# Fewer, fuller tiles of distance bounds, and the first inverse roots ahead of a branch, in a four-layer network on one Trainium2 core

## The chip, the core and the metric

The kernel runs on one core of one Trainium2 chip. Its time is the device time of one execution in microseconds. The time before is 2672.19 us, the median of 3 runs (2671.6 to 2673.48). The engines are called by the names that the profile uses: PE (matmuls), PEld (weight loads), DVE (the vector engine), ACT (the scalar engine), POOL, and SP, which issues the DMAs.

## What is computed

The input is a batch of B = 4 images of 56 x 56 tokens of C = 128 channels. Four layers follow each other: a neighbourhood attention with an MLP, a gated linear recurrence, a softmax attention over the 3136 tokens of an image followed by a mixture of 8 experts, and last an attention by distances followed by an expert choice of 64 experts. The change concerns the distance attention most. The reference computes it in this way:

```python
Q, K, V = (projections of the normalised tokens)
q2 = jnp.sum(Q * Q, axis=-1)
k2 = jnp.sum(K * K, axis=-1)
qk = jnp.einsum('bqd,bkd->bqk', Q, K)
dist2 = q2[:, :, None] + k2[:, None, :] - 2.0 * qk
scores = jnp.exp(-GAMMA * dist2)
attn = jax.nn.softmax(scores, axis=-1)
return jnp.einsum('bqk,bkd->bqd', attn, V)
```

Where all distances are large, every score is the exponential of a very negative number, so all weights of the softmax are equal and the layer adds the mean of V to each token. The kernel takes this short way and proves on the chip that it may: for every pair of a query and a key it bounds the distance from below, by 30 of the 128 channels. If one bound is not large enough, a general version of all layers runs after a second branch. With these inputs it doesn't run.

## The kernel before

**Set-up and branch.** `folded_weights` (L2617 to L2711) loads the weights of the first layers, folds the norm's scale and shift into the projections, centres three 128 x 128 weights (`centred`, L2084), multiplies two of them (`product`, L2094), and bounds the scores of the neighbourhood attention and of the softmax attention. The result is one integer, `safe` (L2709). Every engine reads it and branches (L2710, L2895). The loads are all issued by SP, in program order; the seven groups of image 0, `x[0]`, are the last ones in front of the branch (`fetch`, L148 to L153).

**First layer.** `neighbourhood_of_safe_scores` (L471) works on 28 stripes (4 images, 7 groups of 4 tiles of 112 tokens). The order of PE, DVE and ACT in it is written out by hand. It starts with `ahead(0)` and `ahead(1)`: each takes four pairs of statistics on DVE (L551, L552) and then a chain of 13 small DVE instructions, the inverse roots (`inverse_root`, L875, with `roots`, L541). `first_norm` then normalises the group's four tiles on ACT (L583). `tokens` transposes them (L202) and copies them out (L599), `constants` computes exponentials of small tables on ACT (L784, L789) and `pad_v` on DVE (L785), and `keys` and `queries` make the projections. After that come `ahead(2)`, and the loop over stripes with `ahead(3)` to `ahead(5)` in its first round. DMAs of the constants (`band` to `w_fc2`) are issued behind the branch.

**Softmax attention with pieces beside it.** `Attention.run` (L2002) goes through the images. Per image PE does some 175 products of keys and queries (`s_ps`, L1969), ACT their exponentials (L1976), and PE as many products with the values (`o_ps`, L2052), all on 448 columns in fp32. Between these steps it starts pieces of other layers, by a list of pieces with costs that `Paced` (L1566) spreads over the image; a piece that is marked `apart` is the only one of its list in a step. `background` (L2742) says which pieces stand beside which image: the recurrence beside images 0 and 1; the mixture of experts and the distance layer of images 0 and 1 and the bounds of image 0 beside image 2; the bounds of images 1 and 2, and other pieces, beside image 3. Outside the first layer a scheduler orders the instructions of each engine when the program is built, so that the order on an engine is fixed at run time.

**Bounds.** In `FarAttention.image` (L1711) `products(g)` makes, for group g of 448 tokens, the queries `q_near` (30 channels, repeated in the four quarters of the partitions) and the keys `k_near`: the four tiles of 112 keys of group h lie in the four quarters of 32 partitions, side by side in `k_near[:, h, :]`. `with_norms` (L1757) adds the norms to them. `bounds(g, h)` (L1766) then makes four matmuls (L1772), one from each quarter: 32 rows of 112 keys against 448 queries, in bf16, into four PSUM tiles `d_ps` of 112 x 448. Each is reduced to one column: quarters 0 and 2 by a maximum on DVE (L1777), quarters 1 and 3 on ACT (L1783), by a relu with a sum; with `scalar=True` all are on ACT. An image has 7 x 7 calls, so 196 matmuls and 196 reductions; four images have 784. The PSUM tiles come from a pool of four, which the other pieces share.

**End.** `layers_of_safe_scores` (L2718) splits the bounds of image 3 into halves of two matmuls, in an order in which groups become ready (L2807). Some 21 halves stand beside the last pieces of the mixture and the distance layer, on ACT alone. The rest is handed to `ExpertChoice.experts` (L2296), which spreads them over the 16 lots of experts; per lot PE makes `h_ps` (L2318), ACT copies it (L2325), PE transposes it (L2331), DVE adds a bias (L2334), ACT takes the gelu (L2341), and PE makes the output (L2347). The weights of the lots come by DMA, 1 MB at a time. `decide` (L1830) takes the maximum over everything found. `scatter` adds the results to the tokens and writes the output.

Of the kernel before, what the change touches and what calls it, by code (L numbers as in the profile page):

```python
# [9 lines left out]
F32 = mybir.dt.float32  # L10
# [11 lines left out]
GT = 4  # L22
# [99 lines left out]
NR = 4  # L122
KB, QC = 112, 14
# [3 lines left out]
class Env:  # L127
# [20 lines left out]
    def fetch(self, b, parts=1):  # L148

        n = NT // parts  # L150
        src = self.ins["x"][b].rearrange("(t r) w c -> (r w) t c", r=2)
        for t in range(0, NT, n):
            self.nc.sync.dma_start(self.x[b][:, t : t + n, :], src[:, t : t + n, :])  # L153
# [317 lines left out]
def neighbourhood_of_safe_scores(env: Env, f, work):  # L471
# [17 lines left out]
    with ExitStack() as ctx:  # L489
# [64 lines left out]
        def ahead(i):  # L554

            (b, s), (x, tiles) = stripes[i], tiles_of(i)
            all_of = statistics[b]
            if s == 0:
                all_of["mv"] = sp.tile([P, NT, 2], F32, tag="mv_all", name="mv_all", bufs=2)
            for t in range(tiles.start, tiles.stop):  # L560
                statistic(x, t, all_of["mv"][:, t, :])
            if b == 0:
                held[i]["norm"] = roots(all_of["mv"][:, tiles, :], GT)
            elif s == NG - 1:
                rs, off = roots(all_of["mv"], NT)
                for s2 in range(NG):
                    of = slice(s2 * GT, (s2 + 1) * GT)
                    held[b * NG + s2]["norm"] = rs[:, of], off[:, of]
# [248 lines left out]

        plan = work(ps1, NG + 1)
# [8 lines left out]
        with tc.manual_schedule(  # L827
            engines={mybir.EngineType.PE, mybir.EngineType.DVE, mybir.EngineType.Activation}
        ):
            for i in range(2):  # L830
                ahead(i)
                first_norm(i)
# [787 lines left out]
class FarAttention:  # L1620
# [14 lines left out]

    def __init__(self, env, ctx, flow, work):
# [23 lines left out]
        self.far = cp.tile([P, 1], F32, tag="far", name="far")  # L1660
        self.half = cp.tile([P, 1], F32, tag="half", name="half")


        self.found = cp.tile([P, B * NG * NG * NR], F32, tag="found", name="found")
        self.most, self.sums = 0, B * NG * NG * NR

    def weights(self):
# [31 lines left out]
        def bound():  # L1699
            ps = flow.one([128, 512], "n_ps")  # L1700
            nc.tensor.matmul(ps[:P, :2], env.ones[:, :P], part, start=True, stop=True)
            nc.vector.tensor_reduce(self.far, ps[:P, :2], AX.X, ALU.add)
# [8 lines left out]
    def image(self, b, spans, places="d"):  # L1711
# [8 lines left out]
        def turned(g):  # L1720
            if g == 0:
                held["sums"] = sp.tile([128, NG], F32, tag="x_sums", name="x_sums")
                held["k"] = pool.tile(
                    [128, NG, P], BF16, tag="k_near", name="k_near", bufs=2 if b % 2 else 1
                )
# [8 lines left out]
        def products(g):  # L1734
            square = self.work.tile([128, C * GT], F32, tag=f"xn_{places}", name="square", bufs=1)
            square = square.bitcast(BF16)
            k_square = sp.tile([128, P], BF16, tag=f"square_{places}", name="k_square", bufs=1)
# [5 lines left out]
            for r in range(NR):  # L1743
                nc.tensor.matmul(
                    k_ps[32 * r : 32 * (r + 1), :P], self.k_w,
                    held["xnT"][:, r * P : (r + 1) * P], start=True, stop=True,
# [3 lines left out]
                (q, square[:, :GW], q_ps), (held["k"][:, g, :], k_square, k_ps),  # L1750
# [15 lines left out]
        def bounds(g, h, tiles=range(NR), scalar=False):  # L1766


            found = [flow.one([128, 512], "d_ps")[:P, :GW] for _ in tiles]
            for r, d in zip(tiles, found):  # L1770
                part = slice(32 * r, 32 * (r + 1))
                nc.tensor.matmul(  # L1772
                    d, held["k"][part, h, :], held["q"][g][part, :], start=True, stop=True
                )
            for r, d in zip(tiles, found):
# [5 lines left out]
                else:  # L1781
                    self.sums -= 1
                    nc.scalar.activation(  # L1783
                        d, d, AF.Relu, bias=self.half,
                        accum_out=self.found[:, self.sums : self.sums + 1],
# [20 lines left out]
        def of(span):  # L1806
            take, norm = span_norms(env, sp, b, span, places)

            def tokens(g):
# [15 lines left out]
                costing(1.0, lambda g=g, h=h, *a: bounds(g, h, *a), True)  # L1825
                for g in range(NG) for h in range(NG)
# [3 lines left out]
    def decide(self):  # L1830

        env, nc, sp = self.env, self.env.nc, self.small
        found = sp.tile([P, 2], F32, tag="found", name="found")
# [3 lines left out]
        far = sp.tile([P, 2], F32, tag="is_far", name="is_far")  # L1837
# [6 lines left out]
        nc.tensor.matmul(ps[:1, :2], env.ones[:P, 0:1], far, start=True, stop=True)  # L1844
        count = sp.tile([1, 1], F32, tag="count", name="count")
        nc.vector.tensor_reduce(count, ps[:1, :2], AX.X, ALU.add)
        nc.vector.tensor_scalar(count, count, 2.0 * P - 0.5, None, ALU.is_lt)
# [769 lines left out]
def folded_weights(env: Env, ctx):  # L2617

    tc, nc, ins = env.tc, env.nc, env.ins
    cp = ctx.enter_context(tc.tile_pool(name="w_const", bufs=1))
    f = {}
    f["w"] = w = env.load(cp, "w_qkv", ins["L0_conv_w_qkv"])
    for i, name in enumerate(("b_q", "b_k")):
        f[name] = env.column(cp, name, ins["L0_conv_b_qkv"][i * C : (i + 1) * C])
    f["b_v"] = env.row(cp, "b_v", ins["L0_conv_b_qkv"][2 * C :])
# [5 lines left out]
    safe = cp.tile([1, 1], mybir.dt.int32, tag="safe", name="safe")  # L2633
    with (
        tc.tile_pool(name="w_setup", bufs=1) as up,
        tc.tile_pool(name="w_ps", bufs=2, space=PSUM) as ps,
    ):
        heads = up.tile([128, NH], F32, tag="heads", name="heads")
# [3 lines left out]
        ln_w = env.column(up, "ln_w", ins["L0_conv_ln1_w"])  # L2642
        ln_b = env.column(up, "ln_b", ins["L0_conv_ln1_b"])
        f_ps = ps.tile([128, 512], F32, tag="one", name="f_ps")
        for i in range(2):
# [9 lines left out]
        nc.vector.tensor_scalar(w, w, ln_w, None, ALU.mult)  # L2655

        scale = C**-0.5
        w_q = centred(env, up, "w_q", ins["L2_attn_Wq"])
        w_k = centred(env, up, "w_k", ins["L2_attn_Wk"])
        b_q = env.column(up, "b_q2", ins["L2_attn_bq"])  # L2660
        z_w, z_b = soft["z_w"], soft["z_b"]
        nc.vector.tensor_copy(z_w, product(env, up, ps, "z_w0", w_q, w_k, scale))
        nc.vector.tensor_copy(z_b, product(env, up, ps, "z_b0", w_k, b_q, scale))
        nc.vector.tensor_copy(
            soft["w_out"], value_weights(env, up, ps, ins["L2_attn_Wv"], ins["L2_attn_bv"])
        )

# [3 lines left out]
        nc.vector.tensor_copy(  # L2671
            norms2[:, 0 : 4 * NH], head_norms(env, ps, up, w, f["b_q"], f["b_k"], heads)
        )
        rpb = up.tile([1, NH, K7 * K7], F32, tag="rpb", name="rpb")
        nc.sync.dma_start(rpb, ins["L0_conv_rpb"].unsqueeze(0))
        env.fetch(0, NG)
        nc.vector.tensor_tensor(rpb, rpb, rpb, ALU.mult)
        nc.vector.tensor_reduce(norms2[:, 4 * NH : 5 * NH], rpb, AX.X, ALU.add)
        sq = up.tile([128, C], F32, tag="sq2", name="sq2")
        part = up.tile([128, 2], F32, tag="part2", name="part2")  # L2680
        nc.vector.tensor_tensor(sq, z_w, z_w, ALU.mult)
        nc.vector.tensor_reduce(part[:, 0:1], sq, AX.X, ALU.add)
        nc.vector.tensor_tensor(part[:, 1:2], z_b, z_b, ALU.mult)
        n_ps = ps.tile([128, 512], F32, tag="one", name="n_ps")
        nc.tensor.matmul(n_ps[:1, :2], env.ones[:, 0:1], part, start=True, stop=True)
        nc.vector.tensor_copy(norms2[:, 5 * NH :], n_ps[:1, :2])
        nc.scalar.activation(norms2, norms2, AF.Sqrt)
# [21 lines left out]
        nc.vector.tensor_copy(safe, most)  # L2709
    return f, soft, nc.values_load(safe, min_val=0, max_val=1)  # L2710
# [7 lines left out]
def layers_of_safe_scores(env: Env, f, soft):  # L2718
    with ExitStack() as ctx:
# [74 lines left out]
        def trail(i):  # L2794
# [11 lines left out]

        halves = [  # L2807
            (lambda scalar=False, g=g, h=h, tiles=tiles: bounds[g * NG + h](g, h, tiles, scalar))
            for m in range(NG) for g in range(m + 1) for h in range(m + 1) if m in (g, h)
            for tiles in (range(0, 2), range(2, NR))  # L2810
# [106 lines left out]
```

## Time and profile before

| | |
|---|---|
| median of 3 runs | 2672.19 us |
| the profiled execution | 2678.24 us, of which 2676.4 us are its span |
| first layer, mainly (0 to 690 us) | PE busy 597.3, DVE 587.5, ACT 503.3 us |
| attention, image 2 (1567 to 1994 us) | PE busy 425.3 of 427 us |
| attention, image 3 (1994 to 2440 us) | PE busy 429.2 of 446 us |
| last pieces of image 3 (2440 to 2532 us) | PE busy 65.6 of 92 us |
| experts beside bounds (2532 to 2617 us) | PE busy 75.0, DVE 55.9, ACT 66.1 of 85 us |
| rest of the experts, and output (2617 to 2677 us) | PE busy 32.6 of 60 us |

The stages are windows of the trace; the bounds of one are given by first and last instructions of its lines. The page's section on the chain that ended last is empty for this run, so what bounds a stage has to be read from the timeline and from the waits. In the timeline each row gives the start, the duration, the engine, the line, the operation with output and inputs, the count of merged instructions, and in brackets the idle time before it and what ended it.

### The profile page before, as it was taken

The numbers are of one execution on the slowest core, as the hardware profiler recorded it, in microseconds if no ns is written. First come the engines' busy times: TensorE is split into PE (matmuls) and PEld (weight loads), VectorE is DVE, ScalarE is ACT, GpSimd is POOL, SyncE is SP. The second block draws the span as 40 slices with busy tenths as digits, with TensorE's granted clock in tenths as the row PEclk, the third lists the DMA queues.
The fourth block names the chain that finished last, engine by engine and source line by source line (L and its number), as shares of the span: only waits on it lengthen the run. The fifth ranks groups of instructions, "written<-read, shape, count | busy, mean of one in ns | idle before, by whom it ended". The sixth has DMA issues, their size and how long they took to land.

```text
span 2676.4 us, 40173 instructions
## 1 busy us (share of the span) xinstructions
PE 2478.0 (93%) x14849; PEld 1336.8 (50%) x14849; DVE 2024.6 (76%) x5777; ACT 1690.3 (63%) x3539; POOL 4.3 (0%) x34
## 2 busy tenths in 40 slices
PE   5999988888999999999999999999999998997795
PEld 3777666666544544444454444444444443442333
DVE  7887899998388685879958877854788576767564
ACT  3899777784677774767633366565545665753671
POOL 0000000000000000000000000000000000000000
PEclk8999998998999999999999999999999998997687
DMA  6000000000000000000000000000000000001265
GB/s 134 10 10 2 1 2 2 2 2 1 9 1 1 1 0 1 1 1 1 1 11 0 1 1 1 1 1 1 1 1 1 1 0 1 1 1 76 98 250 181
DMA packets 39923, 54.01 MB, mean 20 GB/s; under 512 B 4104, under 2 KB 35443, under 8 KB 35620
## 3 DMA queue, kind: packets, MB, share of 16 engines
q1 hardware_dynamic: 39716, 51.34, 6.0%
q8 instruction: 119, 1.95, 0.3%
q14 instruction: 88, 0.72, 0.1%
HBM read 44.78 MB, written 6.42 MB: 19 GB/s over the span
## 4 chain that ended last, share of the span: by engine, by line


## 5 line engine op out<-in xcount | busy, mean ns | idle before, releaser
L1969 PE MATMUL s_ps<-zT,xnT 128*128 128x448 f32 (+1 forms) x1400 | 654.3, 559 | 11.6 <-ACT e L1976 11.2
L2052 PE MATMUL o_ps<-e,keep 128*128 128x448 f32 (+1 forms) x1376 | 645.8, 553 | 0.0
L1976 ACT ACTIVATE e<-s_ps 128x448 f32<-128x448 f32 x688 | 363.9, 542 | 444.4 <-PE s_ps L1969 436.3
L1969 PEld LDWEIGHTS s_ps<-zT,xnT 128*128 128x128 f32 (+1 forms) x1400 | 238.5, 189 | 232.3 <-issue 181.5
L2052 PEld LDWEIGHTS o_ps<-e,keep 128*128 128x128 f32 (+1 forms) x1376 | 241.9, 190 | 218.4 <-issue 217.2
L1783 ACT ACTIVATE d_ps<-d_ps,half 112x448 f32<-112x448 f32 x412 | 249.2, 606 | 158.0 <-PE d_ps L1772 156.9
L1777 DVE TENSOR_REDUCE found<-d_ps 112x1 f32<-112x448 f32 x372 | 224.3, 618 | 75.8 <-PE d_ps L1772 72.6
L1513 PE MATMUL y_ps<-experts,xnT 128*112 128x512 f32 x448 | 217.8, 608 | 3.1 <-ACT d_ps L1783 2.1
L1518 DVE TENSOR_TENSOR gated<-y_ps,gate 112x512 f32<-112x512 f32 x224 | 151.7, 687 | 46.7 <-PE y_ps L1513 44.5
L1772 PE MATMUL d_ps<-q_near,k_near 32*112 32x448 bf16 x784 | 154.9, 411 | 15.1 <-ACT d_ps L1783 7.7
L1523 DVE TENSOR_TENSOR gated<-gated 112x512 f32<-112x512 f32 (+1 forms) x336 | 152.8, 463 | 3.3
L202 PE MATMUL xT_ps<-ident,xn 112*128 112x112 f32 x672 | 117.3, 279 | 38.8 <-ACT xn L1613 18.5
L202 PEld LDWEIGHTS xT_ps<-ident,xn 112*128 112x128 f32 x672 | 80.4, 145 | 112.9 <-ACT xn L1613 53.8
L1772 PEld LDWEIGHTS <-k_near 32*112 32x112 bf16 x784 | 47.0, 127 | 179.2 <-issue 166.7
L1513 PEld LDWEIGHTS y_ps<-experts,xnT 128*112 128x112 f32 x448 | 75.8, 179 | 99.4 <-issue 58.3
L768 PE MATMUL f_ps<-w_fc,h 128*112 128x128 f32 x896 | 110.1, 282 | 2.4 <-ACT h L759 1.6
L1613 ACT ACTIVATE xn<-x,g_off,g_rs 112x128 f32<-112x128 f32 x224 | 94.5, 484 | 26.2 <-DVE g_off L1603 9.7
L768 PEld LDWEIGHTS f_ps<-w_fc,h 128*112 128x112 f32 x896 | 104.2, 183 | 7.9 <-ACT h L759 4.5
L583 ACT ACTIVATE xn<-x,off,rs 112x128 f32<-112x128 f32 x224 | 91.6, 481 | 20.8 <-DVE off L546 20.8
L669 DVE TENSOR_TENSOR e<-e,band 112x1792 f32<-112x1792 f32 (+3 forms) x56 | 99.8, 1784 | 0.0
L759 ACT ACTIVATE h<-h_ps,b_fc 128x448 f32<-128x448 f32 x112 | 61.9, 635 | 55.3 <-PE h_ps L754 55.3
L754 PE MATMUL h_ps<-zT,w_fc 128*128 128x448 f32 x224 | 94.9, 569 | 0.6 <-ACT zT L748 0.6
(386 smaller groups left out, 4063.0 us busy)
## 6 DMA issues: line engine op xcount, KB each, us to landing
lot<-in_L_ffn_lots SPq DMA_DIRECT2D x32, 1024.0 KB
out_x<-x SPq DMA_DIRECT2D x28, 224.0 KB
x<-in_x SPq DMA_DIRECT2D x3, 1568.0 KB
x<-in_x SPq DMA_DIRECT2D x7, 224.0 KB
parts<-in_waves SPq DMA_DIRECT2D x8, 173.0 KB
out<-found SPq DMA_DIRECT2D x64, 2.0 KB
w_fc<-in_L_conv_w_fc SPq DMA_DIRECT2D x2, 256.0 KB
experts<-in_L_ffn_expert_w SPq DMA_DIRECT2D x1, 512.0 KB
```

The costliest lines, as they stand in the source:

```text
L202: self.nc.tensor.transpose(ps[:, j * P : (j + 1) * P], xn[:, j, :], self.ident[:P, :P])
L669: nc.vector.tensor_tensor(es, es, bands[stripes[i][1] == 0][:n].rearrange("p h r c -> p h (r c)").unsqueeze(2) .to_broadcast([n, NH, m, 8 ...
L768: nc.tensor.matmul(f_ps[:, j, :], h[:, k, j * P : (j + 1) * P], w_fc2[:, k, :], start=(k == 0), stop=(k == 3),)
L1513: nc.tensor.matmul(y_ps, held["xnT"][g][:, j * P : (j + 1) * P], self.experts[:, 4 * i : 4 * i + 4, :], start=True, stop=True,)
L1518: nc.vector.tensor_tensor(gated[:, some, :], y_ps, gate[:, some].unsqueeze(2).to_broadcast([P, 4, C]), ALU.mult,)
L1523: nc.vector.tensor_tensor(gated[:, :n, :], gated[:, :n, :], gated[:, n : 2 * n, :], ALU.add)
L1772: nc.tensor.matmul(d, held["k"][part, h, :], held["q"][g][part, :], start=True, stop=True)
L1777: nc.vector.tensor_reduce(self.found[:, self.most : self.most + 1], d, AX.X, ALU.max)
L1783: nc.scalar.activation(d, d, AF.Relu, bias=self.half, accum_out=self.found[:, self.sums : self.sums + 1],)
L1969: nc.tensor.matmul(s_ps[i * n : (i + 1) * n, :GW], self.xnT[:, at : at + n], zT, start=True, stop=True,)
L1976: nc.scalar.activation(e[:n], s_ps[:n, :GW], AF.Exp)
L2052: nc.tensor.matmul(sums[:, :GW], self.keep[:n, k, :], e[:n], start=(k == 0 and g - 1 not in pairs), stop=last,)
```

## The change

1. The keys of an image are dealt over the quarters in another way. Groups 0 to 5 lie as before, one behind the other without gaps, in 6 x 112 = 672 columns; the last group gives each quarter 160 columns, which begin 96 tokens apart. So each quarter holds 768 different keys, 6 tiles of 128 columns, and the last quarter 64 more. `bounds(g, c, parts)` takes tile c of 128 keys from each quarter, and c = 6 is the remainder of 64 keys in the last quarter alone, always on ACT. An image has 7 x (6 x 4 + 1) = 175 matmuls, four images 700. The statistics of what was found, and `decide`, are on 128 partitions; `found` is cleared once by POOL.
2. The pieces of the list keep their cost (1.0 for a call of four, 0.25 for the remainder), and an image still has 49 pieces (42 and 7). The halves of image 3 are 91 in place of 98.
3. In front of the branch: group 0 of `x[0]` is loaded first of all, groups 1 and 2 between the weights; groups 3 to 6 move behind the branch, behind the constants of the first layer. The statistics of groups 0 and 1 and their inverse roots (one chain on 8 columns) are computed in front of the branch; `ahead(0)` and `ahead(1)` go. Three centrings move from DVE to ACT, two copies on DVE go, and the order of PE, DVE and ACT in the set-up is written by hand.

```diff
+NC = NG * P // 128
+LP = NC * 128 - (NG - 1) * P
+LW = GW - (NR - 1) * LP
...
+        env.fetch(0, range(3, NG))
         plan = work(ps1, NG + 1)
...
+            rs, off = f["roots"]
             for i in range(2):
-                ahead(i)
+                held[i]["norm"] = (a[:, i * GT : (i + 1) * GT] for a in (rs, off))
                 first_norm(i)
...
+            n, step = (P, P) if g < NG - 1 else (LW, LP)
...
-                    k_ps[32 * r : 32 * (r + 1), :P], self.k_w,
-                    held["xnT"][:, r * P : (r + 1) * P], start=True, stop=True,
+                    k_ps[32 * r : 32 * (r + 1), :n], self.k_w,
+                    held["xnT"][:, r * step : r * step + n], start=True, stop=True,
...
-        def bounds(g, h, tiles=range(NR), scalar=False):
-            found = [flow.one([128, 512], "d_ps")[:P, :GW] for _ in tiles]
-            for r, d in zip(tiles, found):
+        def bounds(g, c, parts, scalar=False):
+            scalar = scalar or c == NC
+            n = 128 if c < NC else LW - LP
+            found = [flow.one([128, 512], "d_ps")[:n, :GW] for _ in parts]
+            for r, d in zip(parts, found):
                 part = slice(32 * r, 32 * (r + 1))
                 nc.tensor.matmul(
-                    d, held["k"][part, h, :], held["q"][g][part, :], start=True, stop=True
-                )
+                    d, held["k"][part, 128 * c : 128 * c + n], held["q"][g][part, :],
+                    start=True, stop=True,
+                )
...
+    env.fetch(0, [0])
     f["w"] = w = env.load(cp, "w_qkv", ins["L0_conv_w_qkv"])
...
+        w_q, w_k = (env.load(up, f"w_{i}", ins[f"L2_attn_W{i}"]) for i in "qk")
+        b_q = env.column(up, "b_q2", ins["L2_attn_bq"])
+        env.fetch(0, [1])
+        w_v = env.load(up, "w_v", ins["L2_attn_Wv"])
+        rpb = up.tile([1, NH, K7 * K7], F32, tag="rpb", name="rpb")
+        nc.sync.dma_start(rpb, ins["L0_conv_rpb"].unsqueeze(0))
+        b_v = env.row(up, "b_v2", ins["L2_attn_bv"], 128)
+        env.fetch(0, [2])
...
+        def centred_by_scalar(w):
+            minus = up.tile([128, 1], F32, tag="minus", name="minus", bufs=3)
+            nc.scalar.activation(sq, w, AF.Identity, scale=-1.0 / C, accum_out=minus)
+            nc.scalar.activation(w, w, AF.Identity, bias=minus)
...
+        statistics_of(range(GT))
...
+        statistics_of(range(GT, 2 * GT))
...
+        inverse_root(env, up, mv[:, :, 1], rs)
+        nc.vector.scalar_tensor_tensor(off, mv[:, :, 0], -1.0, rs, ALU.mult, ALU.mult)
+        f["roots"] = rs, off
```

## The prediction

> **What bounds the kernel now.** I read the page first, its sums and its groups:
>
> ```profile
> PE 2478.0 (93%) x14849; PEld 1336.8 (50%) x14849; DVE 2024.6 (76%) x5777; ACT 1690.3 (63%) x3539; POOL 4.3 (0%) x34
> ...
> L1783 ACT ACTIVATE d_ps<-d_ps,half 112x448 f32<-112x448 f32 x412 | 249.2, 606 | 158.0 <-PE d_ps L1772 156.9
> L1777 DVE TENSOR_REDUCE found<-d_ps 112x1 f32<-112x448 f32 x372 | 224.3, 618 | 75.8 <-PE d_ps L1772 72.6
> ...
> L1772 PE MATMUL d_ps<-q_near,k_near 32*112 32x448 bf16 x784 | 154.9, 411 | 15.1 <-ACT d_ps L1783 7.7
> ```
>
> PE is busy 93% of the span, and 425 of 427 us in the attention of image 2. The bounds take 155 us of PE, 224 of DVE and, with the reading of the accumulator (82.7 us more), about 330 of ACT. A ninth of them goes (84 of 784). So the question is what a bound costs in the stage it lies in; there are three, and the timeline of each answers it.
>
> *The front* (0 to 45 us) is a chain of waits, on DVE and ACT:
>
> ```profile
> 14.30 0.14 DVE L2709 CAST safe<-most 1x1 int32<-1x1 f32 x1
> 15.20 0.29 DVE L551 BATCH_NORM_STATS2 st<-x 112x6 f32<-112x128 f32 x1 [0.76 <-DVE safe L2709]
> ...
> 20.08 1.65 ACT L583 ACTIVATE xn<-x,off,rs 112x128 f32<-112x128 f32 x4 [6.72 <-DVE off L546]
> ...
> 24.25 1.65 ACT L583 ACTIVATE xn<-x,off,rs 112x128 f32<-112x128 f32 x4 [2.53 <-DVE off L546]
> ...
> 25.80 0.51 ACT L599 COPY xnT<-xT_ps 128x448 f32<-128x448 f32 x1
> 26.33 1.28 ACT L784 ACT_TABLE_LOAD   x1
> ```
>
> Behind the branch ACT waits for DVE's two chains of roots; the copy of the first group's tokens stands behind both groups on ACT, and starts at 25.80. Then come the table, pad_w and, at 27.96, pad_v on DVE. From there DVE has no gap up to 44.87, where it releases PE (the transposed bias, on which PE waits 5.5 us). So all that follows hangs on the time of pad_v.
>
> *The attention of images 2 and 3* is bound by PE. PE alone, between 2067 and 2069 us:
>
> ```profile
> 2067.13 0.40 PE L1772 MATMUL d_ps<-q_near,k_near 32*112 32x448 bf16 x2
> 2067.45 1.02 PE L2052 MATMUL o_ps<-e,keep 128*128 128x448 f32 x2
> 2068.40 0.42 PE L1772 MATMUL d_ps<-q_near,k_near 32*112 32x448 bf16 x3
> 2068.76 1.02 PE L1969 MATMUL s_ps<-zT,xnT 128*128 128x448 f32 x2
> ```
>
> Two bounds hold the next matmul up by 0.32 us, three by 0.36: bounds of different quarters run at the same time.
>
> *The experts* (2532 to 2615 us) are bound by the reductions of the last image's bounds. ACT, at 2594 us:
>
> ```profile
> 2594.59 0.61 ACT L1783 ACTIVATE d_ps<-d_ps,half 112x448 f32<-112x448 f32 x1
> 2595.12 0.19 ACT L1783 ACTIVATION_READ_ACCUMULATOR d_ps<-d_ps,half 112x1 f32 x1
> 2595.32 0.61 ACT L1783 ACTIVATE d_ps<-d_ps,half 112x448 f32<-112x448 f32 x1
> ```
>
> One half (a reduction each on DVE and ACT) takes 0.73 us here, 0.70 on average from 2593.17 to 2596.66. A lot with 20 bounds beside it takes 10 to 11.5 us; the lots after the last bound take about 4.1 (their copies stand at 2624.67 and 2628.78).
>
> **The change, part by part.** The sums are made in the profiled execution's time (2678.24 us, span 2676.4) and taken off the median of 2672.19, 6 us below it.
>
> *1. Front.* Removed behind the branch: two calls of `ahead`, 15.20 to 24.14 on DVE. ACT then starts its eight normalisations at about 15.2 and needs 8 x 1.65/4 = 3.3 us, so the copy of 25.80 comes at 18.5: 7.3 us earlier, and with it the table, pad_w and pad_v. That holds if three things don't eat it.
> - The branch. DVE's work in front of it: statistics of 8 tiles, 3.1 us (4 take 1.6); a chain of roots on 8 columns, 2.5 to 3.1 (the two of before; 8 columns for 4 cost the same in the rows of L887); the folding, as before; the bound, 1.05 (13.39 to 14.44). Centring and two copies go to ACT, idle there until 13.13: its six instructions of 128 x 128 that lie before the roots are near the row of k_near's cast (0.27 to 0.28 us), with accumulators 0.2 more. What decides is group 1 of `x[0]`: SP issues it at about 5.4 us, behind 0.22 MB of group 0 and 0.4 MB of weights. The windows show 59 GB/s up to 4 us, 87 up to 8, and 239 after that, with tiny columns slowing the start; so it lands at 8 to 10. DVE reaches it at 8.6 (the folding ends with PE at 7.0, as before, and 1.6 more). Then 1.6 + 0.5 + 2.6 + 1.05 makes `safe` at 14.4, against 14.44; at the latest 16. I take no shift. [...]
> - Groups 3 to 6 now stand on SP's queue behind `w_fc2` (20.66), with 1.25 MB ahead of them since 15.25. At the 140 GB/s of the windows up to 26 us, group 3 lands at 25.7; DVE wants it at 20.9 + 4.2 = 25.1 (one `ahead` is 4.18 us). So 0.6 us are lost, between 0 and 2. Groups 4 and 5 have 4.2 us more each. What is queued behind these four on SP (taps, gates, images 1 to 3, the waves) comes 2 us later; the waves are wanted at 78.19 before, 71 after, and the first ones land by about 62 by the bytes moved. Nobody waits.
> - Band and pad_w: issued at 15.25 to 16.4, wanted at 20.3; 0.42 MB at 142 GB/s lands at 19. Hidden.
>
> POOL gets a clearing of 128 x 700 at some 1300 us; that of q, 128 x 496, is 0.5 us, and nothing is queued behind it that matters. Sum of the front: -6.7, between -8.1 and -3.5.
>
> *2. Attention of images 2 and 3* (bounds of images 0 to 2: 588 matmuls, 525 after). By the mean of the starts in the trace a bound costs PE 0.162 us, so 63 of them would give 10.2. But listing the starts by runs of bounds shows where that comes from: from the first bound of a run to the next other matmul pass 0.333 us for one and the same for two, 0.375 for three, 0.548 for four (median 0.374; the rest is waiting for a free PSUM tile); and the matmul before and the one after it take 0.10 us more each than without a break. [...] That speaks against this change: what costs is the break, not the bound, and an image keeps 49 pieces. The order on PE in the two builds has 238 runs before (64 of one, 66 of two, 40 of three, 68 of four) and 233 after (84, 60, 35, 54). That is 95.6 us before and 28.0 + 20.0 + 13.1 + 29.6 = 90.7 after, and 5 x 0.2 for the neighbours: -5.9. Lower bound of the gain: 5 breaks at 0.53, -2.7; upper: the 10.2, and waits that go with the reductions. A matmul of 128 keys streams the same 448 columns as one of 112, and a reduction reads 448 from each partition either way (e<-s_ps, 128 x 448: 542 ns, d_ps 606 on 112, with a bias); I take no difference, at most 0.02 us each, 1 us in all. DVE loses 42 reductions (26 us) and ACT 21 there; they were not last, PE was. The statistics of a last group on 160 columns for 112 cost 0.05 us, three times.
>
> *3. Experts.* The first 21 halves, on ACT alone beside the last pieces, are of the same number and size: nothing. Left are 77 halves before and 70 after. ACT has one reduction for each, also for the seven remainders: 7 x 0.71 = -5.0. DVE loses 14, but is not last. The order on PE shows the same: bounds end one lot earlier, 20 beside it go, 11 against 4 us. Between -3 (remainders, single, wait for PE each) and -6.7. What is late next is the lots' weights: 32 of 1 MB, nine ahead; DMA is at 44 to 52% from 2590 to 2620 us, so there is room.
>
> Sum: -6.7 - 5.9 - 5.0 = -17.6. 2672.2 - 17.6 = **2654.6 us** (a profiled execution of 2660.6).
>
> **The rivals.**
> - *More than counted* (chance 0.17, about 2644): fewer reductions shorten the waits in the stream. Before bounds PE sits idle 15.1 us; at 2228 us a wait of 2.7 us for ACT is followed by 17 us at half clock (the window 2200 to 2250 has PEclk 0.80), 8.5 us lost. Without that and 2 us of the waits: -28. Against it: the order around that place hardly changes.
> - *Less than counted* (0.16, about 2664): group 1 or 3 of `x[0]` comes late, so the front gives 1; only the breaks count in the attention, 2.7; the experts give 4.5. Together -8.2.
> - *Slower* (0.05, about 2681): the new order in images 2 and 3 leaves PE waiting for operands more than about 2.7 us at places where it did not, and each such wait is followed by a half-clocked stretch as the one at 2228. One costs 2.7 + 8.5 = 11.2; from the second on the gain is gone, three make +16, four +27. For +9 it takes some 2.4 of them. For it: image 3's attention ends in such waits already (PE is 429 of 446 us busy). Against it: all waits over 1.3 us in images 2 and 3 before are two, and the change takes work from DVE and ACT.
>
> That the bounds of the remainder break the stream 28 times more is excluded by the count of runs.
>
> **How the numbers follow.** Likeliest, with 0.62: 2654.6, by its bounds 2648 to 2661. The range takes in most of both neighbours: 2642 to 2666. About 0.2% (5 us) is what a measurement of this kernel can tell from no change. Faster by more: 0.90 (the first two and most of the third); within: 0.05; slower: 0.05.
>
> **What would show it.** Front: first L583 row on ACT at 15 to 16 us, pad_v at 20 to 22, PE's release at 37 to 39; `safe` later than 16.5 or a DVE wait for x over 2 us would be the error. Attention: as many breaks as counted, a run of one to three still 0.32 to 0.37 us, images 2 and 3 shorter by some 6 us together; by 10 or more, and bounds do cost by number. Experts: n_ps (the last bound's count) some 5 us earlier behind the first h_ps, and lots without bounds at 4.1 us. PEclk at half in a new place of images 2 or 3 would make the forecast wrong by 8 us for each.

## The result, and the profile after

The changed kernel takes 2640.78 us, the median of 4 runs (2638.79 to 2641.8), against 2672.84 us of 4 runs of the kernel before (2671.6 to 2677.5). The ratio is 0.9874, with a 95% interval of 0.986 to 0.9889: 32 us faster. The prediction was 2654.6 us, 17.6 us faster, with a range of 2642 to 2666. The sign and the places were right, the gain forecast is little more than half of the gain measured, and the time lies 1.2 us below the range. A later sample of the same kernel gave 2637.0 us, ratio 0.9855 (0.984 to 0.987).

The profiled execution took 2638.79 us, with a span of 2636.9. These are the sums of the page after, and its groups of the bounds:

```profile
PE 2453.5 (93%) x14765; PEld 1319.2 (50%) x14765; DVE 1989.2 (75%) x5689; ACT 1674.5 (64%) x3500; POOL 5.0 (0%) x35
...
L1798 ACT ACTIVATE d_ps<-d_ps,half 128x448 f32<-128x448 f32 (+1 forms) x384 | 232.2, 606 | 120.1 <-PE d_ps L1786 118.0
L1792 DVE TENSOR_REDUCE found<-d_ps 128x1 f32<-128x448 f32 x316 | 190.9, 620 | 73.0 <-PE d_ps L1786 70.8
...
L1786 PE MATMUL d_ps<-q_near,k_near 32*128 32x448 bf16 (+1 forms) x700 | 138.2, 371 | 10.1 <-ACT d_ps L1798 4.0
```

Against the rows of before, a reduction of 128 partitions costs what one of 112 did (606 and 620 ns, against 606 and 618). The matmul of a bound does not: 371 ns in place of 411 (the "+1 forms" are the remainders of 64 keys; the 672 matmuls of 128 keys alone have a mean of 370). I had taken both as equal.

The front, in the timeline after:

```profile
14.38 0.14 DVE L2763 CAST safe<-most 1x1 int32<-1x1 f32 x1
15.17 3.19 ACT L586 ACTIVATE xn<-x,first_off,first_rs 112x128 f32<-112x128 f32 x8 [3.45 <-DVE s_w_out L2764]
...
18.26 0.51 ACT L602 COPY xnT<-xT_ps 128x448 f32<-128x448 f32 x1
...
21.31 0.28 DVE L788 SCALAR_TENSOR_TENSOR pad_v<-pad_w,b_v 49x128 f32<-49x128 f32 x1 [5.58 <-ACT pad_w L787]
```

`safe` stays where it was, the eight normalisations follow each other without a gap, the copy stands at 18.26 (25.80 before) and pad_v at 21.31 (27.96). PE is released at 38.41, 6.7 us earlier than at 45.07.

**Where the rest came from.** To compare traces, I cut them at four matmuls that all of them have: the first output of the MLP (`f_ps`), the first `z_ps` of an image in the attention (the product that makes a group's queries, L1945 before; it is issued some steps ahead of its group), the `z_ps` of image 3's last group, and the first `h_ps` of the experts. In the two traces, from the first `z_ps` of image 3 to that of its last group 503.7 us pass before and 480.7 after. This stretch alone gives 23 us; it holds 360 of the bounds before and 320 after. From the first `h_ps` to the end it is 144.1 and 138.3 us. From the first `z_ps` of image 0 to that of image 2 nothing changes (680.7 and 681.0), and from the last `z_ps` to the first `h_ps` little does (181.0 and 179.6).

The profiled executions stand 39.5 us apart, 7 more than the medians. 5 of these lie in the first layer (597.9 and 592.9 us from the first MLP output to the attention), where both kernels issue the same instructions in the same order. What belongs to the change can't be told from one trace of each.

### The profile page after: what moved, and what is told of

Read it like the earlier page. It is cut to its first block, busy times and chain, and to the rows that moved or that the text cites. A ratio compares the mean times of both kernels' runs of the same rounds, so it can differ in the third digit from the quotient of the medians.

```text
span 2636.9 us, 39881 instructions
## 1 busy us (share of the span) xinstructions
PE 2453.5 (93%) x14765; PEld 1319.2 (50%) x14765; DVE 1989.2 (75%) x5689; ACT 1674.5 (64%) x3500; POOL 5.0 (0%) x35
## 4 chain that ended last, share of the span: by engine, by line
## 5 line engine op out<-in xcount | busy, mean ns | idle before, releaser
L1798 ACT ACTIVATE d_ps<-d_ps,half 128x448 f32<-128x448 f32 (+1 forms) x384 | 232.2, 606 | 120.1 <-PE d_ps L1786 118.0
L1792 DVE TENSOR_REDUCE found<-d_ps 128x1 f32<-128x448 f32 x316 | 190.9, 620 | 73.0 <-PE d_ps L1786 70.8
L1523 DVE TENSOR_TENSOR gated<-y_ps,gate 112x512 f32<-112x512 f32 x224 | 151.9, 688 | 39.8 <-PE y_ps L1518 37.5
L1786 PE MATMUL d_ps<-q_near,k_near 32*128 32x448 bf16 (+1 forms) x700 | 138.2, 371 | 10.1 <-ACT d_ps L1798 4.0
L1786 PEld LDWEIGHTS <-k_near 32*128 32x128 bf16 (+1 forms) x700 | 33.4, 92 | 167.8 <-issue 154.8
```

The lines of the kernel that those rows point to most:

```text
L1523: nc.vector.tensor_tensor(gated[:, some, :], y_ps, gate[:, some].unsqueeze(2).to_broadcast([P, 4, C]), ALU.mult,)
L1786: nc.tensor.matmul(d, held["k"][part, 128 * c : 128 * c + n], held["q"][g][part, :], start=True, stop=True,)
L1792: nc.vector.tensor_reduce(self.found[:, self.most : self.most + 1], d, AX.X, ALU.max)
L1798: nc.scalar.activation(d, d, AF.Relu, bias=self.half[:n], accum_out=self.found[:n, self.sums : self.sums + 1],)
```

## Experiments

Each time is given beside that of before in the same sample, and the ratio is between these two. "Before" and "after" in a diff's heading are the two kernels, and the edits are shown in part. The first five experiments put each part, and each property of a bound, by itself.

**front_alone**: before, with part 3 of the change only (the hunks of the set-up, `fetch` and `ahead`).

> The kernel before with the third part of the change alone (loads, statistics and roots in front of the branch); the bounds stay in 784 tiles of 112 keys. The two traces show pad_v and the first mlp output 7.3 us earlier, and another 5 us that came in the first layer, between 211 and 690 us, where the order of instructions is the same. If the 5 us belong to the one execution that was profiled (its half-clock windows fell badly; it stood 5.4 us above the median), this kernel is 7.3 us faster, 2665.5 us. If they come with the new front, it is 12 us faster, 2660.5 us. If the front also changes what happens in images 2 and 3, it is more.

Measured: 2670.07 us of 15 runs against 2671.7, ratio 0.9989 (0.998 to 0.9998). In its trace the first MLP output comes 7.2 us earlier and the end 12.8 us earlier, but the median gives 1.6, so neither of the two expected times came.

**tiles_alone**: before, with parts 1 and 2 of the change only.

> The kernel before with the first and second part of the change alone (700 bounds of 128 keys); the set-up stays. If the gains add up, it has what front_alone lacks of 32 us: 24.7 us faster, 2648 us, if the front is worth 7.3. My prediction's two terms for it were 10.9 us, which would be 2662 us.

Measured: 2646.12 us, ratio 0.9905 (0.989 to 0.992), 25.6 us below 2671.7. So by far the most is in the bounds.

**wide_keys**: 128 keys to a tile, all 784 bounds kept.

```diff
-                    [128, NG, P], BF16, tag="k_near", name="k_near", bufs=2 if b % 2 else 1
+                    [128, NG, 128], BF16, tag="k_near", name="k_near", bufs=2 if b % 2 else 1
...
-                    held["xnT"][:, r * P : (r + 1) * P], start=True, stop=True,
+                    held["xnT"][:, min(r * P, GW - 128) : min(r * P, GW - 128) + 128], start=True, stop=True,
```

> The kernel before, but every tile of keys has 128 columns in place of 112: the first tokens of the four tiles of a group are 0, 112, 224 and 320, so some keys are bounded twice. 784 bounds, the same pieces, the same order on every engine. Theory of the weights: in the traces a run of bounds held PE up by 0.322 us with 112 keys and 0.288 with 128, because the weights of 128 columns load faster; with some 238 runs that alone gives 8 us, so 2664.8 us, and runs of 0.288 to 0.30 us in the trace. Theory of the number: 84 fewer bounds and reductions gave the gain; then this kernel, which has all of them, stays at 2672.8 us or goes 1 to 2 us above.

Measured: 2662.24 us, ratio 0.9965 (0.9952 to 0.9979), 9.5 us below 2671.7, where 8 were expected of the weights: their theory holds for this kernel.

**narrow_keys**: 112 keys to a tile, with the 700 bounds of after.

```diff
-            n = 128 if c < NC else LW - LP
+            n = P if c < NC else LW - LP
```

> The kernel after, but each bound takes only the first 112 of the 128 keys of its tile (it leaves out the bounds of 16 keys in 128). 700 bounds, the same order on every engine as after. Theory of the weights: the fast load is lost, 0.034 us at each of some 233 runs, 8 us, so 2648.8 us and runs of 0.322 us. Theory of the number: all 84 are still gone, so 2640.8 us as after.

Measured: 2642.73 us, ratio 0.989 (0.9875 to 0.9905). Against the two ratios of after, 0.9874 and 0.9855, the faster weights are worth 4 to 9 us here, so the 8 of their theory is not excluded. In either case their part is the smaller one: 29 us are left without them. The number is the larger.

What the weights do is seen in the groups of weight loads and matmuls of a bound, each shape by itself. The kernel before, then wide_keys, then keys_of_120 (the experiment that follows):

```profile
L1772 PE MATMUL d_ps<-q_near,k_near 32*112 32x448 bf16 x784 | 154.9, 411 | 15.1 <-ACT d_ps L1783 7.7 <-DVE found L1777 4.9 <-DVE gated L1518 0.3
L1772 PEld LDWEIGHTS <-k_near 32*112 32x112 bf16 x784 | 47.0, 127 | 179.2 <-issue 166.7 <-DVE x L1998 2.0 <-DVE g_st L1596 1.9
```

```profile
L1772 PE MATMUL d_ps<-q_near,k_near 32*128 32x448 bf16 x784 | 144.8, 377 | 16.2 <-ACT d_ps L1783 8.3 <-DVE found L1777 5.0 <-DVE gated L1518 0.4
L1772 PEld LDWEIGHTS <-k_near 32*128 32x128 bf16 x784 | 34.4, 92 | 179.9 <-issue 166.6 <-DVE g_st L1596 2.0 <-DVE x L1998 2.0
```

```profile
L1773 PE MATMUL d_ps<-q_near,k_near 32*120 32x448 bf16 x784 | 154.4, 409 | 15.7 <-ACT d_ps L1784 7.9 <-DVE found L1778 5.2 <-DVE gated L1518 0.3
L1773 PEld LDWEIGHTS <-k_near 32*120 32x120 bf16 x784 | 47.8, 129 | 176.7 <-issue 164.7 <-DVE x L1999 2.0 <-DVE g_st L1596 1.3
```

A load takes 127 ns with 112 columns, 129 with 120, and 92 with 128.

**keys_of_120**: wide_keys with 120 in place of 128.

> wide_keys with 120 columns of keys to a tile in place of 128 (784 bounds, the order of before). A single bound held PE up by 0.302 us with 64 columns, 0.322 with 112 and 0.288 with 128. If only full weights of 128 columns load fast, and the rest pay by the column (0.020 us for 48), a run of one takes 0.325 us here, more than with 112; if it were a matter of more columns for the same keys or of alignment, it lies between 0.288 and 0.322 us.

Measured: 2672.58 us (one run). By the starts in the trace, a single bound holds the next matmul up by 0.322 us with 112 columns, 0.325 with 120 and 0.288 with 128. So of the three widths only the full 128 columns gains; 120 columns load no faster than 112.

The next question was whether the number counts by PE's matmuls or by the reductions.

**unread**: before, with all 784 matmuls, but three results of four of the last key group are not reduced.

```diff
             for r, d in zip(tiles, found):
+                if h == NG - 1 and r < NR - 1:
+                    continue
```

> The kernel before with all of its 784 bounds, of 112 keys, but the results of three of the four tiles of the last key group are not reduced (it leaves out 84 reductions, 56 of DVE and 28 of ACT, as many as the change takes away). Theory of the reductions: what made images 2 and 3 shorter by 16 us without the faster weights is that DVE and ACT have less to reduce, so tiles come free earlier and the wait of 2.68 us for ACT with its 17 us at half clock is not there; then image 3 is some 12 to 18 us shorter here too, the time is about 2672 - 18 (attention) - 5 (experts) = 2649 us, and no wait over 2 us stands in image 3. Theory of the matmuls: the gain came from 84 fewer matmuls and 5 fewer breaks on PE; then images 2 and 3 stay as before, only the experts gain 5, and the time is 2667 us.

**reread**: after, but each remainder is reduced twice by DVE and twice by ACT.

```diff
+            for d in found if c == NC else []:
+                for _ in range(2):
+                    nc.vector.tensor_reduce(
+                        self.found[:n, self.most : self.most + 1], d, AX.X, ALU.max
+                    )
+                    self.most += 1
...
+                    if c == NC:
+                        self.sums -= 1
+                        nc.scalar.activation(
+                            d, d, AF.Relu,
+                            accum_out=self.found[:n, self.sums : self.sums + 1],
+                        )
```

> The kernel after with its 700 bounds, but every remainder of 64 keys is reduced four times (twice by DVE, twice by ACT) in place of once, so DVE and ACT have 784 reductions again, as before. PE has the work of after. Theory of the reductions: images 2 and 3 lose most of what the number of bounds gave, 12 to 16 us, a wait over 2 us with half clock behind it comes back in image 3, and the experts lose 5: 2641 + 19 = 2660 us. Theory of the matmuls: only the experts lose 5: 2646 us.

**after_again**: the changed kernel, unchanged.

> The changed kernel once more, for its ratio to before in this call and a second trace. Order and work are the same, so 2640.8 us. If half-clock windows of the first layer differ from execution to execution, the first layer (first mlp output to the start of the attention) differs by up to 5 us from the 592.9 us of the first trace, and the windows lie at other places; if they follow from the program, both traces agree within 0.5 us.

Measured: unread 2654.72 us, ratio 0.9924 (0.9911 to 0.9938); reread 2656.37 us, 0.9928 (0.9915 to 0.9942); after_again 2637.0 us, 0.9855. So 84 reductions less, with as many matmuls on PE, give 20 us, and 84 reductions more take 19 from after. The times speak for the reductions, though neither kernel changes them alone. With less or more to reduce, the scheduler also orders PE in another way: the bounds of images 0 to 2 lie in 221 runs in unread (238 before) and in 239 in reread (233 after), which by the prediction's prices of runs and breaks is an estimated 6 of the 20 us and 2 of the 19. And in reread four reductions read one PSUM tile one behind the other (609, 609, 591 and 520 ns), which keeps it from the next matmul for longer. The road of the gain is not the one that I expected, as the rows of the image-3 stretch show (start and end, length, busy time of PE, PEld, DVE, ACT and POOL, then PEclk, DMA share and GB/s). Before, unread, reread, narrow_keys, after:

```profile
1847.60:2351.30 503.70, 493.41 (x1747) 211.13 (x1746) 365.40 (x1137) 298.41 (x770) 0.00 (x0) 0.98 0.00 1
```

```profile
1844.30:2334.40 490.10, 481.25 (x1747) 207.12 (x1746) 354.26 (x1113) 289.33 (x746) 0.00 (x0) 1.00 0.00 1
```

```profile
1837.60:2327.30 489.70, 480.73 (x1707) 203.78 (x1706) 362.35 (x1135) 296.19 (x766) 0.00 (x0) 1.00 0.00 1
```

```profile
1840.30:2328.10 487.80, 481.97 (x1702) 208.13 (x1701) 350.48 (x1110) 288.45 (x742) 0.00 (x0) 0.98 0.00 1
```

```profile
1838.20:2318.90 480.70, 474.39 (x1701) 202.52 (x1700) 349.98 (x1110) 288.67 (x742) 0.00 (x0) 0.99 0.00 1
```

Against this trace of before, unread and reread both shorten it by about 14 us, one with fewer reductions and one with fewer matmuls and faster weight loads; both together give 23. What they have in common stands in the last columns: PEclk 1.00. The trace's clock record has 23.9 us at half clock in this stretch before, and 3.4 in each of these two. Half clock is the only lower clock in it, and costs nearly half of PE's speed: in the trace of before a pair of matmuls of the gate (`l_ps`, L2208) takes 0.97 us at full clock (at 2213.37) and 1.75 at half (at 2232.57). Before has one wait of 2.68 us there. reread has none over 1 us, though all its reductions are back. So my mechanism, reductions that make this one wait, is not what the runs show.

**joined**: after, with the remainder copied to all four quarters, so that four groups' remainders run side by side in one piece.

```diff
-                for c, parts in enumerate([range(NR)] * NC + [[NR - 1]])
+                for c, parts in enumerate([range(NR)] * NC + of_rest(g))
...
+        def of_rest(g):
+            return [range(min(NR, NG - g))] if g % NR == 0 else []
```

> The kernel after with the remainder of 64 keys copied to all four quarters, so that the remainders of four groups of queries, then of three, are one piece of bounds that run side by side (two pieces per image for seven; half of their reductions go to DVE). 700 bounds still. By the cost of a break (0.29 us for the run and 0.2 for its neighbours), 15 pieces fewer in images 2 and 3 give 7 us; in the experts 4 halves for 7 take 3 x 0.7 = 2 us off ACT: 2632 us. If PE does not gain where pieces are fewer, because the scheduler splits the fours again, or if new waits come, it stays at 2640 us.

Measured: 2642.69 us, ratio 0.9879 (0.9864 to 0.9894), no faster than after. In the image-3 stretch PE has 142 runs of bounds in place of 149, but waits 7.9 us in place of 6.3, and 17.1 us are at half clock in place of 6.8. It saves the breaks, and has more waits and half clock in their place; the expected 2632 us did not come.

Next come second traces of before and of its new front, and the experts.

> The kernel before, unchanged, for a second trace. If the profiled execution of before (2678.24 us, 5.4 us above its median) was long by its half-clock windows in the first layer, this one has a first layer (first mlp output to the start of the attention) shorter than 597.9 us, near 592 to 595, and the same front (first mlp output at 90 us), the same wait of 2.68 us for the normalised tokens in image 3, and 17 us of half clock behind it.

before_again: 2674.68 us (one run); first layer 592.9 us; image-3 stretch 509.0 us, with 37.5 us at half clock. Here is the wait in its timeline:

```profile
2222.88 0.96 PE L2208 MATMUL l_ps<-zT,gate_w 128*64 128x448 f32 x2
2226.53 0.82 PE L202 MATMUL xT_ps<-ident,xn 112*128 112x112 f32 x3 [2.68 <-ACT xn L1613]
```

> front_alone once more (the new set-up with the old bounds). Its trace had the first output of the mlp 7.2 us earlier, but its median was only 1.6 us below before (interval 0.5 to 5.3). If the front is worth what the trace shows, 7.2 us, and the first sample fell badly in its half-clock windows, this one stands 5 to 9 us below before; if something behind the front gives 5 us back in most executions, it stands 1 to 3 us below before again, and a trace of such an execution shows where (a longer first layer or a longer image 3).

front_again: 2672.01 us of 21 runs against 2673.95, ratio 0.9987 (0.9978 to 0.9997). Its trace: first MLP output 6.3 us earlier than before, first layer 598.0 us, image-3 stretch 505.7. So the same program takes between 592.8 and 598.0 us for the first layer, and between 503.7 and 509.0 for the image-3 stretch; each of the two programs showed both ends of the first.

**rest_on_vector**: after, with the seven remainders beside the experts on DVE.

```diff
-            scalar = scalar or c == NC
+            scalar = scalar or c == NC and b < B - 1
...
-                if r % 2 == 0 and not scalar:
+                if (r % 2 == 0 or c == NC) and not scalar:
```

> The kernel after, but the remainders of image 3 that stand beside the experts are reduced by DVE in place of ACT (7 reductions move; nothing is left out). If ACT's reductions bound the experts, as the prediction took it, 7 x 0.71 = 5 us go: 2634 us by the mean of the two medians of after (2640.8 and 2637.0). If DVE and ACT bound them alike, or the lots' own steps do, it stays at 2637 to 2641 us.

Measured: 2638.24 us, ratio 0.9868 (0.9853 to 0.9883), inside the two medians of after. The experts from the first `h_ps` to the last reduction, after and then rest_on_vector (columns as above):

```profile
2498.60:2568.40 69.80, 64.87 (x583) 24.46 (x581) 45.60 (x84) 58.38 (x162) 0.00 (x0) 0.89 0.70 258
```

```profile
2501.40:2571.40 70.00, 65.40 (x583) 24.41 (x581) 48.74 (x89) 54.97 (x149) 0.00 (x0) 0.87 0.71 257
```

ACT loses 3.4 us of work and the stretch stays at 70 us. PE is the busiest engine in both.

The last two ask whether the single wait carries the gain. Both kernels are before without eight bounds of the third image, at the place of the wait and behind it.

```diff
         def bounds(g, h, tiles=range(NR), scalar=False):
+            if b == 2 and g == 2 and h < 2:
+                return
```

> The kernel before without eight of its 784 bounds: two calls of four (queries of group 2, key groups 0 and 1 of the third image), which stand at the place of the wait in image 3. The order on PE differs in a few rows around that place and nowhere else. Eight bounds and their two breaks are worth 1 to 2 us by their slots. If the single wait of 2.68 us with its half clock carries a large part of the gain, it is gone or below 2 us here, image 3 has some 14 us less at half clock, and the time is 8 to 12 us below before (2662 to 2666 us). If the gain is spread over image 3, the time is 1 to 3 us below before (2671 us).

> The same with two other calls (queries of group 5, key groups 0 and 1 of the third image), which stand behind the place of the wait. The wait of 2.68 us and its half clock are still there, so 1 to 2 us below before, by both theories (2672 us); more only if breaks at this later place start a half-clocked stretch of their own.

Measured: eight_out 2669.35 us of 14 runs, ratio 0.9989 (0.9979 to 1.0); eight_out_late (with `g == 5`) 2670.85 us, 0.9995 (0.9985 to 1.0005), both against 2673.36. In eight_out's trace the wait is gone; the longest one of the stretch is this:

```profile
2233.73 4.09 PE L1971 MATMUL s_ps<-zT,xnT 128*128 128x448 f32 x6 [1.25 <-ACT e L1978]
```

and from the fifth `z_ps` of the image to the sixth, where the wait stood, 6.8 us are at half clock, against 17 to 21 in four traces of 784 bounds. This part is 95.6 us long against 99.7 to 102.2. Yet the time falls by 2.9 us (ratio; 0 to 5.6), not by 8 to 12, and the control does not differ from it beyond the intervals. The theory of the single place falls.

The wait is not even what starts the half clock in every trace. In wide_keys the matmuls in front of the wait are slow already (1.75 us in place of 0.97):

```profile
2218.86 1.75 PE L2208 MATMUL l_ps<-zT,gate_w 128*64 128x448 f32 x2
2223.28 1.38 PE L202 MATMUL xT_ps<-ident,xn 112*128 112x112 f32 x6 [2.68 <-ACT xn L1613]
```

And before_again goes to half clock at 1873.6 us behind 6.9 us in which PE is busy throughout. These are the rows of that stretch and of the next one (columns as above):

```profile
1866.70:1873.60 6.90, 6.90 (x33) 3.80 (x31) 4.31 (x13) 4.65 (x13) 0.00 (x0) 1.00 0.01 2
1873.60:1883.80 10.20, 10.20 (x30) 5.18 (x30) 3.06 (x11) 4.91 (x14) 0.00 (x0) 0.50 0.00 0
```

## Why the prediction missed

**The front: right.** The first MLP output comes at 90.6 us on average in eight traces with the old set-up (89.7 to 92.1) and at 84.0 in eight with the new one (83.1 to 84.9): -6.6 for a forecast of -6.7. `safe` did not move, group 3 was there when DVE asked at 25.68, and the bounds I gave held. Group 1 let DVE wait for 0.26 us, at 8.45, so the windows' rate was near. The tiny columns that I named as slowing the start take SP 0.42 to 0.43 us each to issue in the trace of before (four of 0.5 KB from 1.21 to 3.51 us), as long as the 192 KB of `w_qkv` (0.41). What the front is worth in the time stays open: the two samples of the front alone give 1.6 and 1.9 us (intervals reach to 5.3 and 5.9), on top of the new tiles it looks like more (0.9905 against 0.9874 and 0.9855). The first layer behind it varies by 5 us from execution to execution, and no trace shows where a fixed share would be lost.

**The attention: the term that failed.** The prediction took -5.9 for the bounds of images 0 to 2: breaks saved, at the old cost of a run. The breaks came as counted (238 and 233 runs), but the two stretches lose 22.7 us together, far over the 10 at which, by the prediction's own sign, bounds do cost by number. Three steps failed: each run length kept its old cost, a load of 128 columns was taken to cost what one of 112 does, and waits and half clock were left out of the sum.

The stretch of image 2 measures +1.4 (478.6 in the four traces with the old bounds that are named below, 480.0 on average in after, after_again, tiles_alone and rest_on_vector). Its runs of bounds, each measured from its first bound to the next other matmul, take 2.3 us less (26.4 and 24.1), but three of the four new traces have half clock there (6.8, 3.4 and 6.8 us; after_again has none, nor has any of the old). This is one of the new places that the prediction feared, at 2.1 us on average. The rest, +1.6, I can't place.

The stretch of image 3 measures -24.1: 503.7, 509.0, 505.7 and 505.7 in before, before_again, front_alone and front_again, 480.7, 481.5, 482.3 and 483.0 in the same four of the new bounds. I split these by the trace's records:
- *Half clock*: 30.4 us in the first four on average, 10.2 in the second. With half of each such microsecond counted as lost, an estimate from the 0.97 and 1.75 us above, this is -10.1. I had it as a rival ("more than counted", 0.17, 2644 us), tied to one wait; the runs show it spread, and eight_out shows that this wait alone does not carry it. The size is uncertain, since half clock scatters: 23.9 to 37.5 us in the four old traces and 6.8 to 13.7 in the four new ones, but 16.9 in keys_of_120 with its 784 bounds and 17.1 in narrow_keys with 700.
- *The slots of the bounds* (the runs, measured as above), at full clock (a half-clocked microsecond counted half): 60.7 us in 155 runs before (mean of before and before_again), 51.8 in 149 after: -9.0. narrow_keys has 54.8, so -5.9 is the number and -3.0 the weights. The prediction multiplied new run counts with old run costs. Runs of four did not keep theirs: in this stretch 0.60 us before, 0.50 in narrow_keys. Fewer reductions in front of the next free tile are not the whole reason, since unread has as few and its runs of four still take 0.60; what is stays open. And I wrote that "a matmul of 128 keys streams the same 448 columns as one of 112", which is so, but its weights load in 92 ns and not 127.
- *Breaks*: 6 fewer, at 0.2 for the neighbours: -1.2. This, and the claim that a break costs and not a bound, held for short runs: those of one, two and three before cost 0.32, 0.33 and 0.36 us here. Why PE loses time at a break is not shown.
- What is left, -3.8, I put down to the waits of other matmuls, without having parted it further: PE is idle 10.3 us in the stretch before and 6.3 after, some of it within the slots above.

I had written that reductions do not count here, since "they were not last, PE was". A PE that is 98% busy still waited 10 us, and the times of unread and reread speak for what reductions cost. The two do not add up. Counted at full clock, the stretch is 490.8 us on average in the first four traces, 488.4 in unread, 488.0 in reread and 476.8 in the four of the new bounds. So what unread and reread gain in this stretch is nearly all half clock, which each of their traces has in 3.4 us only; at full clock each gives 2 to 3 us, and both changes together 14. Why they give so much more together is not shown.

**Experts: size nearly right, by luck.** -6.8 on average (144.1 and 143.2 in before and before_again, 138.3 and 135.5 in after and after_again), for -5.0 (-3 to -6.7). But the last bound's count (`n_ps`) comes 13.1 us earlier behind the first `h_ps` in the first pair (84.5 and 71.4) and 9.8 in the second, not 5. In the first pair 6.5 of the 13.1 are half clock (29.9 and 16.8 us of it, counted at half), and 7.3 are lost again in the lots behind it. rest_on_vector moved seven reductions off ACT, and nothing followed, so that ACT's reductions bound this stretch is not what the runs show. What does is open; PE, busy for 65 of 70 us at a clock of 0.89, is the nearest.

**The sum.** -6.6 + 1.4 - 24.1 - 6.8 = -36.1, to set against -32.1 and -37.8 in the two samples of after. The range missed since half clock and fewer waits stood in a rival of 28 us alone, and the range ended 2 us beyond it.

Not shown: what takes the 10 us of half clock away. Fewer waits are a likely reason by my estimate, since seven traces of the last section have 13.7 to 20.5 us of it around one wait, but not a sufficient one: two of the traces above go to half clock ahead of a wait or without one, and narrow_keys, where PE is idle for 5.8 us of the stretch, has 17.1 us at half clock, while reread, with 9.0 us idle, has 3.4.

## What to carry to other kernels

When work is taken from engines that are not last, do not put its worth at nothing: here 84 reductions, with the order on PE that came with them, made some 20 us beside a PE that was 98% busy in the stretch that gained most. Price a changed shape on each instruction that it touches, the weight load too; here the step from 112 to 128 columns made a load a quarter shorter (127 and 92 ns). And before a difference of a few microseconds is explained, take a second trace of the same program: two stretches here varied by 5 us without any change.

## What the runs showed of the hardware that I had not expected

- The same instructions in the same order take 592.5 to 598.0 us in the first layer, in 16 traces, with 34.9 to 54.6 us at half clock from the first MLP output on. Nearly all half clock comes in pieces of 3.4 us and multiples (3.4, 6.8, 10.2, 13.7, 17.1, and up to 30.7 in before and after); other lengths stand only at the end of a trace (13.5 us in before, 14.2 in after).
- In image 3 much of it lies around one wait. In seven traces (before, before_again, front_alone, front_again, wide_keys, keys_of_120, eight_out_late) 13.7 to 20.5 us at half clock lie around a wait of 2.67 or 2.68 us; around a wait of 2.09 us at the same place, in unread, there are none. In two of the seven the half clock begins clearly ahead of the wait, by 0.5 us in eight_out_late and by 1.7 in wide_keys.
- It comes without a gap too. Image 2 of after goes to half clock at 1583.8 and 1648.6 us, and before_again at 1873.6, each behind 6.8 or 6.9 us of a busy PE. after_again has the same instructions at the first two places and stays at full clock. In all three, transposes and matmuls of 8 columns (the router's) stand in front; whether they are the reason, no run here tests.
- In the trace of after, half clock begins at 2198.2 us, at the end of this row of short waits:

```profile
2194.93 0.34 PE L1786 MATMUL d_ps<-q_near,k_near 32*64 32x448 bf16 x1 [0.46 <-DVE best L2232]
...
2196.60 0.97 PE L2227 MATMUL l_ps<-zT,gate_w 128*64 128x448 f32 x2 [0.62 <-ACT zT L2222]
2197.50 0.36 PE L1786 MATMUL d_ps<-q_near,k_near 32*128 32x448 bf16 x3
2198.57 0.53 PE L1786 MATMUL d_ps<-q_near,k_near 32*128 32x448 bf16 x1 [0.71 <-DVE found L1792]
```

- Half the columns of weights do not halve a load: in after, one of 64 columns takes 103 ns, more than one of 128 (91), and a single bound of 64 keys holds PE up by 0.302 us, against 0.288 for one of 128.
